# Pattern stage of a four-layer graph network: degrees as column sums on TensorE, five generators in flight in another order, mask buffers at other addresses

## The chip, the core and the metric

The kernel runs on one core of one Trainium2 chip. A core has TensorE (PE, with its weight loads listed apart as PEld), VectorE (DVE), ScalarE (ACT), GpSimd (POOL) and SyncE (SP), which here issues most transfers. The metric is the device time of one execution in microseconds, as the median of several runs.

## The reference, cut to what matters

The input is 16 graphs of 1024 nodes with 128 features each, and a sparse, symmetric adjacency matrix per graph. Four layers follow, each with a residual and a layer norm: graph attention, three SAGE convolutions on a thinned ("dilated") adjacency, and two plain graph products. The part that concerns us is the thinning, which goes row by row, since each row's removals change the later rows:

```python
def step(carry, n):
    row = jnp.take(carry, n, axis=0)
    nbi = row.astype(jnp.int32)
    num = jnp.sum(nbi)
    sf = jnp.where(num > T_DIL, (num + K_DIL - 1) // K_DIL, 1)
    rank = jnp.cumsum(nbi)
    rm = row & (rank % sf == 0)
    valid = (mask_b[n] != 0) & (num > 1)
    rm = jnp.where(valid, rm, False)
    keep = ~rm
    carry = carry.at[n].set(row & keep)
    carry = carry.at[:, n].set(carry[:, n] & keep)
    return (carry, None)
out, _ = jax.lax.scan(step, adj_bool, jnp.arange(N))
```

Here T_DIL is 10 and K_DIL is 2. The convolution then uses `adj * keep`, its row sums as degrees, three times with weights of its own and a batch norm over all nodes:

```python
deg = jnp.clip(jnp.sum(adj, axis=-1, keepdims=True), 1.0, None)
agg = jnp.einsum('bij,bjd->bid', adj, x) / deg
out = agg @ Wr + x @ Wx + b
```

## The kernel before

The program has four stages in one TileContext: `phase_att` (attention, layer 0), `phase_pattern` (the thinning), `phase_conv` (the three convolutions) and `phase_end` (layers 2 and 3). Memory is taken in pools. A pool opened after another one was closed gets the bytes of the closed one, and its tiles wait for the closed one's users. The code gives the order of instructions, but a planner that looks at the whole program with estimated times may let an instruction go ahead of older ones on its engine, within what the rings of buffers allow.

**Attention** writes for each graph a 0/1 mask of the adjacency in f16 (`MT` in SBUF, then `mask_d` in device memory, L261 to 272) and the layer's output `x1_d`, also transposed as `x1T_d`. `finish` of the last graph (L477) is the stage's tail. Its last steps are the reduction of `seen_z` into a flag (L589) and the stores of `x1_d` and `x1T_d` (L530 to L540).

**The pattern stage** uses that almost all nodes have few neighbours: of a sparse graph only nodes with 10 or more neighbours (candidates, at most 128 per graph) can lose edges. There are three kinds of generators.

- `find(b)`, one for each of 16 graphs, 11 yields. It loads the mask `m` (2 MB, a ring of three buffers, L726) and sums its rows on ACT with eight Relu instructions that accumulate (L730); that gives the degrees. POOL multiplies the eight diagonal blocks by a triangle (`md`, L734). Three times `earlier` follows (36 one-column matmuls, L744 and L748), with a comparison on DVE between, which finds the nodes that are small with respect to earlier ones. `slots` gives each candidate a slot and builds a one-hot `oh` (L700). `nodes` finds the node of each slot (8 matmuls, L710) and its indices (five operations on DVE, L713 to L717), and starts a gather of the nodes' features on POOL (L718). A second gather fetches the nodes' rows of the adjacency (`rows`, L776). Then come `pg` (64 matmuls, L785, the last readers of `m`) and `stay`, `le`, `l2` and `base` on DVE (L793 to L798), `pr` (L802) with RB, `early` and `num0` (L803 to L808), the transposes of the gathered rows (`pt`, L815) and their product with the one-hot (`pv`, L821, copied to `V`).
- `settle(g)`, one for eight graphs, 8 yields: five rounds that iterate the removals of eight graphs at once. Each is about ten tiny operations and three wide ones on DVE (L844 to L859), then eight one-column matmuls (L862). After them come the products `py` and `pk`, the edge weights `d`, and a store to `slots_d` (L912).
- `alone(b)`, one for each graph, 4 yields: ranks all nodes against the candidates (`prank`, 12 matmuls, L923), marks hits with two comparisons on DVE (`hit1` L928, `hit` L930), and finds small nodes whose edges are all gone, with `slots`, `nodes` and one more gather (L947).

The function `rolling(tasks, depth, lag)` (L624) writes these generators out in turns: one step of each that is active, in the order of their start. A further one starts when fewer than `depth` are active, the youngest has done `lag` steps, and those named as its conditions have ended. Before the change the call is `rolling(tasks, 3, 4)`. The list is: finds 0 to 7, settle 0, finds 8 to 15, settle 1, alones 0 to 7, alones 8 to 15 (which wait for settle 1).

PSUM is used through two rings of the stage: `ps` (four small tiles: all short sums, `pc`, `pr`, `pv`, `pn`) and `pb` (two wide tiles: `pg`, `pt`, `prank`, and the wide ones of `settle`).

**The convolution** starts on PE when its own pools are free and its first loads have landed; its first use of POOL is the power in `norm` (L1148).

Of the kernel before, what the change touches and what calls it, by code (L numbers as in the profile page):

```python
# [10 lines left out]
F32 = mybir.dt.float32  # L11
# [6 lines left out]
ALU = mybir.AluOpType  # L18
# [125 lines left out]
def phase_att(ctx, tc, t, c, x1_d, x1T_d, mask_d, flags):  # L144
# [13 lines left out]

    k_rank = load("k_rank", [P, E])
# [4 lines left out]
    k_id = load("k_id", [P, W])  # L164
    k_id_col = load("k_id_col", [P, 1])
    off_diag = cp.tile([P, W], F16, name="off_diag")
# [8 lines left out]
    w_all = cp.tile([P, 4 * F], F32, name="w_all")  # L175
    bias3 = cp.tile([P, 4 * F], BF16, name="bias3")
# [48 lines left out]

    MT = [cp.tile([P, NG, (NG - 1) * W + P], F16, name=f"mask{i}") for i in range(2)]
    for m in MT:
        nc.gpsimd.memset(m, 0.0)
    QS = [cp.tile([P, UNITS, C], F16, name=f"qs{i}") for i in range(2)]
    for q in QS:  # L230
        nc.gpsimd.memset(q, 0.0)
# [413 lines left out]
def phase_pattern(ctx, tc, t, c, mask_d, slots_d, x1_d, keep, flags):  # L645
# [5 lines left out]
    nc = tc.nc  # L651
    cp = ctx.enter_context(tc.tile_pool(name="q_c", bufs=1))
    mp = ctx.enter_context(tc.tile_pool(name="q_m", bufs=3))
# [6 lines left out]
    def load(name, shape, dtype=F16):  # L660
        w = cp.tile(shape, dtype, name=name)
        nc.sync.dma_start(w, t[name])
        return w
# [9 lines left out]
    node_col = node[:, :, 0]  # L673

# [7 lines left out]
    v2 = cp.tile([P, B], F32, name="v2")  # L682
    small = cp.tile([P, B, T], F16, name="small")
    seen_slots = cp.tile([P, 2 * B], F32, name="seen_slots")
# [7 lines left out]
    def slots(k, chosen, upto):  # L692
# [4 lines left out]
        slot = sm.tile([P, T], F16, name="slot")  # L697
# [6 lines left out]
        nc.vector.tensor_reduce(seen_slots[:, k : k + 1], slot, AX.X, ALU.max)  # L704
        return oh

    def nodes(k, oh, pc):
# [4 lines left out]
        at = sm.tile([P, 3], F32, name="at")  # L712
        nc.vector.tensor_scalar(at[:, 0:1], pc, -1.0, 0.0, op0=ALU.add, op1=ALU.max)  # L713
        nc.vector.tensor_scalar(at[:, 2:3], pc, 0.0, float(N), op0=ALU.is_equal, op1=ALU.mult)
        nc.vector.tensor_scalar(keep.index[:, k : k + 1], at[:, 0:1], float(k % B * N), None, op0=ALU.add)
        nc.vector.tensor_copy(keep.inner[:, k : k + 1], at[:, 0:1])
        nc.vector.tensor_tensor(keep.row[:, k : k + 1], at[:, 0:1], at[:, 2:3], ALU.add)  # L717
# [5 lines left out]
    def find(b):  # L723
# [3 lines left out]
        deg = sm.tile([P, T], F32, name="deg")  # L727
        for ti in range(T):
# [225 lines left out]
    for g in range(2):  # L954
        tasks += [(f"f{b}", find(b), []) for b in range(g * HALF, (g + 1) * HALF)]
        tasks.append((f"s{g}", settle(g), [f"f{b}" for b in range(g * HALF, (g + 1) * HALF)]))
        if g:
            tasks += [(f"a{b}", alone(b), []) for b in range(HALF)]
# [1206 lines left out]
```

## Time and profile before

| | us |
|---|---|
| median of 3 runs | 3310.53 (3309.57 to 3317.0) |
| profiled execution | 3305.06 |
| its span | 3303.3 |
| attention's last sums copied (L473) | 1711.4 |
| attention's last transposes done on PE | 1727.5 |
| first load of the pattern stage | 1734.9 |
| first `earlier` matmul (L748) | 1757.2 |
| settle 0, first operation and end | 1885.3, 1931.1 |
| settle 1, about, and end | 2045.5, 2091.7 |
| last `nodes` (L710) | 2182.4 |
| first product of the convolution (L1115) | 2191.4 |
| mean TensorE clock granted over the span | 0.917 |

Times on the profile's axis count from the start of the span. An idle time is put down to the event that came last before the engine went on; where the engine or tensor named had nothing to do with it, it was another. Busy times of PE include the pipelining of matmuls, so a share near 80% of PE means some 20% of real gaps, and a share of one engine over a stretch says nothing of which stage within it waits.

### The profile page before, as it was taken

To read this page: it belongs to the slowest core of one execution; us is meant where nothing else is said; L and a number is where in the kernel's file an instruction comes from. 1 tells how busy PE (TensorE), PEld (TensorE's weight loads), DVE (VectorE), ACT (ScalarE), POOL (GpSimd) and SP (SyncE) were. 2 spreads that over 40 slices of the span, in tenths; PEclk is the share of its full clock that TensorE was granted. 3 is DMA by queue.
4 is the path that set the end of the run, shared out by engine and by line. 5 is a ranking of instruction groups with operands and counts; after the bars stand their busy time and mean duration, and the time that the engine had idled before them with its cause. 6 is when DMAs were issued, how large, how long until landed. Compare 5 with 4: busy or idle time off the path is not lost. (4 is left out here: it accounts for less than half of the span.)

```text
span 3303.3 us, 68844 instructions
## 1 busy us (share of the span) xinstructions
PE 2837.5 (86%) x24700; PEld 2493.6 (75%) x24700; DVE 2312.2 (70%) x8374; ACT 1857.5 (56%) x5704; POOL 1351.8 (41%) x1302
## 2 busy tenths in 40 slices
PE   3999999999999999999975667567877799999997
PEld 1878887788877888778865666346766799999997
DVE  3788888888888888888763666755655466666665
ACT  1777777777777777777756733025645333333332
POOL 7655455554545545544023322133423333332221
PEclk7999999999999999999986867679989899999999
DMA  4422332223322233221015532034442444444341
GB/s 124 126 79 77 96 95 70 77 76 96 95 64 83 76 96 96 71 77 43 21 33 185 164 106 88 13 105 145 156 174 107 162 168 168 150 168 162 131 158 40
DMA packets 162014, 348.47 MB, mean 105 GB/s; under 512 B 14708, under 2 KB 68230, under 8 KB 161536
## 3 DMA queue, kind: packets, MB, share of 16 engines
q1 hardware_dynamic: 150912, 315.57, 29.9%
q0 software_dynamic: 10752, 28.42, 3.1%
q8 instruction: 197, 3.23, 0.4%
q14 instruction: 153, 1.25, 0.1%
HBM read 257.87 MB, written 87.03 MB: 104 GB/s over the span
## 5 line engine op out<-in xcount | busy, mean ns | idle before, releaser
L268 POOL TENSOR_SCALAR mask<-ld 104x1024 f16<-104x1024 f32 (+1 forms) x160 | 463.6, 2898 | 331.7 <-PE pg L428 170.9
L423 PE MATMUL pg<-parts,oh 104*128 104x384 f32 x1760 | 558.6, 392 | 0.3 <-ACT hg L442 0.2
L455 PE MATMUL pa<-hg,we 128*104 128x129 f32 (+1 forms) x3520 | 550.2, 274 | 3.5 <-ACT hg L442 2.3
L436 DVE SCALAR_TENSOR_TENSOR junk<-pg,w_a 128x128 f32<-128x128 f32 x1600 | 403.5, 284 | 204.0 <-PE pg L428 201.0
L442 ACT ACTIVATE hg<-pg,hg 128x128 f32<-128x128 f32 x1600 | 510.3, 369 | 16.5
L455 PEld LDWEIGHTS pa<-hg,we 128*104 128x104 f32 x3520 | 493.3, 173 | 22.2 <-ACT hg L442 10.4
L428 PE MATMUL pg<-parts,oh 104*128 104x384 f32 x1760 | 496.2, 353 | 0.0
L428 PEld LDWEIGHTS pg<-parts,oh 104*128 104x128 f32 x1760 | 320.4, 191 | 1.2
L423 PEld LDWEIGHTS pg<-parts,oh 104*128 104x128 f32 x1760 | 285.9, 192 | 28.4 <-issue 4.4
L440 ACT ACTIVATE hg<-sc 128x2 f32<-128x2 f32 (+1 forms) x880 | 186.7, 212 | 173.9 <-DVE junk L436 170.8
L410 DVE TENSOR_TENSOR we<-k_id,ids 128x832 f32<-128x832 f16 (+1 forms) x240 | 249.1, 1038 | 5.7 <-PE pa L455 3.6
L380 ACT CAST oh<-oh_b 104x1024 fp32r<-104x1024 bf16 (+1 forms) x240 | 223.2, 969 | 16.7 <-DVE oh_b L376 16.2
L1294 POOL TENSOR_TENSOR rstd<-ve,mhalf 128x4 f32<-128x4 f32 x96 | 97.0, 1011 | 326.2 <-DVE ve L1293 326.2
L287 PE MATMUL pw<-w_all,xT 128*104 128x512 f32 x320 | 178.8, 643 | 11.4 <-DMA xT<-in_xTp 8.9
L490 POOL TENSOR_TENSOR own<-parts 104x128 f32<-104x128 f32 x160 | 90.6, 600 | 220.4 <-DVE x_rows L510 208.7
L327 DVE TENSOR_TENSOR g<-k_slot,off 105x1408 f16<-105x1408 f16 x80 | 133.0, 1662 | 57.0 <-ACT off L323 57.0
L1298 DVE TENSOR_SCALAR x<-x,mv,rstd 128x128 f32<-128x128 f32 x256 | 106.9, 459 | 88.7 <-POOL rstd L1294 88.7
L376 DVE TENSOR_TENSOR oh_b<-pw,k_slot_edge 104x512 bf16<-104x512 f32 (+1 forms) x240 | 147.0, 636 | 9.5 <-PE pw L375 8.6
L348 ACT CAST qs<-pw 104x416 f16<-104x416 f32 (+1 forms) x240 | 114.6, 478 | 63.5 <-PE pw L345 62.2
L730 ACT ACTIVATE junk<-m 128x1024 bf16<-128x1024 f16 x128 | 133.6, 1048 | 29.2 <-POOL md L734 18.9
L355 DVE SCALAR_TENSOR_TENSOR one_way<-qs,mask 104x1040 bf16<-104x1040 f16 (+9 forms) x160 | 147.5, 922 | 1.1 <-POOL mask L270 0.7
L1403 ACT ACTIVATE y<-x,shift,rstd 128x128 f32<-128x128 f32 x128 | 52.7, 482 | 162.9 <-POOL shift L1396 162.9
(348 smaller groups left out, 6889.8 us busy)
## 6 DMA issues: line engine op xcount, KB each, us to landing
ld<-in_adjT SPq DMA_DIRECT2D x144, 416.0 KB
m<-mask_d SPq DMA_DIRECT2D x16, 2048.0 KB
keep_adj<-in_adjT SPq DMA_DIRECT2D x8, 4096.0 KB
adj<-in_adjT SPq DMA_DIRECT2D x8, 4096.0 KB
mask_d<-mask SPq DMA_DIRECT2D x144, 208.0 KB
hT_d<-uT SPq DMA_DIRECT2D x48, 512.0 KB
h<-hT_d SPq DMA_DIRECT2D x48, 512.0 KB
hT<-hT_d SPq DMA_DIRECT2D x32, 512.0 KB
```

Source lines behind the costliest of these rows:

```text
L268: nc.gpsimd.tensor_scalar(mt[:n, s, :N], ld[:n], 0.0, None, op0=ALU.is_gt)
L287: nc.tensor.matmul(pw[:W], xT[:, s * W : (s + 1) * W], w_all, start=True, stop=False)
L355: nc.vector.scalar_tensor_tensor(junk[:W, :nb, :], q[:W, at : at + nb, :W], EDGE, mt[:W, i, i * W : NP].rearrange("p (n w) -> p n w", w=W) ...
L376: nc.vector.tensor_tensor(o[:W, n0 : n0 + m, 1, :], pw[:W, :m, :], k_slot_edge[:W].unsqueeze(1).to_broadcast([W, m, C]), ALU.is_equal,)
L380: nc.scalar.copy(wide.ends[:W, n0 : n0 + m], o[:W, n0 : n0 + m])
L410: nc.vector.tensor_tensor(we[:, :n, :], k_id.unsqueeze(1).to_broadcast([P, n, W]), wide.ids[:, 2 * lo : 2 * hi].unsqueeze(2).to_broadcast( ...
L423: nc.tensor.matmul(flat[:, : 3 * F], own, d.parts[i][:W, p, :], start=p == 0, stop=False, skip_group_check=True,)
L428: nc.tensor.matmul(pg[:, 1:, :], other, reversed_parts(d.parts[j][:W, p, :]), start=False, stop=p == 1, skip_group_check=True,)
L436: nc.vector.scalar_tensor_tensor(junk, pg[:, 1 + e, :], 0.0, w_a2, op0=ALU.max, op1=ALU.mult, accum_out=d.sc[:, at + e : at + e + 1],)
L440: nc.scalar.activation(hg[:, u - lo, :ways, F], d.sc[:, at : at + ways], AF.Exp)
L442: nc.scalar.activation(hg[:, u - lo, e, :F], pg[:, 3 - 3 * e, :], AF.Copy, scale=hg[:, u - lo, e, F : F + 1])
L455: nc.tensor.matmul(PA[bank][:W, at : at + part.stop - part.start], we[:, 2 * (u - lo) + e, :], hg[:, u - lo, e, part], start=False, stop=T ...
```

## The change

Seven edits, all but the first and the last in `phase_pattern`:

- In attention, the tiles `MT` and `QS` come first in the constants' pool, then the constants that only the early part of a graph's work reads; `k_id` and those read to the end come after.
- The constants of the pattern stage go to a pool `q_k` of their own, and this and the masks' pool `q_m` (still three buffers) are opened first, so that they get the lowest addresses.
- `find` yields after the load. Then it forms the degrees as column sums of the mask on PE: for each of eight column blocks eight matmuls with a column of ones (64 in all), since the matrix is symmetric. One copy on ACT brings them to SBUF.
- `le` becomes eight Sign activations on ACT (values −1 and 1 in place of 0 and 1); `l2` carries twice the edge constant, and RB and `early` add `num0` and halve.
- In `alone`, `hit1` becomes a Sign on ACT. The slots of all calls are kept in one tile and checked at the end instead of one reduction per call.
- `nodes` keeps one operation on DVE in place of five. The others are done for eight graphs at once (`inner`), in `settle` and after the last `alone`; the gathers of features move to `alone` and to the end of the stage.
- The tasks' order is: finds 0 to 9, settle 0, then finds 10 to 15 alternating with alones 0 to 5, settle 1, alones 6 and 7, alones 8 to 15. The call is `rolling(tasks, 5, 2)`. The pools `late`, `xs` and `ahead` move to the other side of memory.

```diff
+    MT = [cp.tile([P, NG, (NG - 1) * W + P], F16, name=f"mask{i}") for i in range(2)]
+    for m in MT:
+        nc.gpsimd.memset(m, 0.0)
+    QS = [cp.tile([P, UNITS, C], F16, name=f"qs{i}") for i in range(2)]
...
     k_slot_edge = load("k_slot_edge", [P, C], F32)
-    k_id = load("k_id", [P, W])
     k_id_col = load("k_id_col", [P, 1])
+    w_all = cp.tile([P, 4 * F], F32, name="w_all")
+    bias3 = cp.tile([P, 4 * F], BF16, name="bias3")
...
+    k_id = load("k_id", [P, W])
...
+    kp = ctx.enter_context(tc.tile_pool(name="q_k", bufs=1))
+    mp = ctx.enter_context(tc.tile_pool(name="q_m", bufs=3))
     cp = ctx.enter_context(tc.tile_pool(name="q_c", bufs=1))
-    mp = ctx.enter_context(tc.tile_pool(name="q_m", bufs=3))
...
+    half_up = cp.tile([P, T], F32, name="half_up")
+    nc.vector.tensor_scalar(half_up, node_col, -1.0, 0.5, op0=ALU.mult, op1=ALU.add)
...
-        nc.vector.tensor_reduce(seen_slots[:, k : k + 1], slot, AX.X, ALU.max)
...
-        at = sm.tile([P, 3], F32, name="at")
-        nc.vector.tensor_scalar(at[:, 0:1], pc, -1.0, 0.0, op0=ALU.add, op1=ALU.max)
-        nc.vector.tensor_scalar(at[:, 2:3], pc, 0.0, float(N), op0=ALU.is_equal, op1=ALU.mult)
-        nc.vector.tensor_scalar(keep.index[:, k : k + 1], at[:, 0:1], float(k % B * N), None, op0=ALU.add)
-        nc.vector.tensor_copy(keep.inner[:, k : k + 1], at[:, 0:1])
-        nc.vector.tensor_tensor(keep.row[:, k : k + 1], at[:, 0:1], at[:, 2:3], ALU.add)
+        first = float(k % B * N)
+        nc.vector.tensor_scalar(
+            keep.index[:, k : k + 1], keep.node[:, k : k + 1], first - 1.0, first, op0=ALU.add, op1=ALU.max
+        )
+
+    def inner(k0, k1):
+
+        k = slice(k0, k1)
+        at = sm.tile([P, HALF], F32, name="at")
+        none = sm.tile([P, HALF], F32, name="none")
+        nc.vector.tensor_scalar(at, keep.node[:, k], -1.0, 0.0, op0=ALU.add, op1=ALU.max)
+        nc.vector.tensor_scalar(none, keep.node[:, k], 0.0, float(N), op0=ALU.is_equal, op1=ALU.mult)
+        nc.vector.tensor_copy(keep.inner[:, k], at)
+        nc.vector.tensor_tensor(keep.row[:, k], at, none, ALU.add)
+
+    def rows_of_x1(k):
         nc.gpsimd.indirect_dma_start(
             keep.xs[:, k, :], None, x1_d[k % B],
...
         nc.sync.dma_start(m, mask_d[b].rearrange("(t p) n -> p t n", p=P))
-        deg = sm.tile([P, T], F32, name="deg")
-        for ti in range(T):
-            junk = wp.tile([P, N], BF16, name="junk")
-            nc.scalar.activation(junk, m[:, ti, :], AF.Relu, accum_out=deg[:, ti : ti + 1])
-        yield
+        yield
+
+        pu = ps_s.tile([P, T], F32, name="pu", tag="ps")
+        for ni in range(T):
+            for ci in range(T):
+                nc.tensor.matmul(
+                    pu[:, ni : ni + 1], m[:, ci, ni * P : (ni + 1) * P], one, start=ci == 0, stop=ci == T - 1
+                )
+        deg = sm.tile([P, T], F32, name="deg", bufs=6)
+        nc.scalar.copy(deg, pu)
...
+        le = wp.tile([P, T, P], F16, name="le", bufs=3)
+        for ti in range(T):
+            nc.scalar.activation(le[:, ti, :], row, AF.Sign, bias=half_up[:, ti : ti + 1])
         yield
...
-        le = wp.tile([P, T, P], F16, name="le")
-        nc.vector.tensor_tensor(le, node_col.unsqueeze(2).to_broadcast([P, T, P]), row_b, ALU.is_le)
+        nc.vector.tensor_tensor(base[:, b], pg, stay, ALU.mult)
         l2 = L2[b % 2]
-        nc.vector.scalar_tensor_tensor(l2[:, :, :P], oh, EDGE, le, op0=ALU.mult, op1=ALU.add)
-        nc.vector.tensor_tensor(base[:, b], pg, stay, ALU.mult)
+        nc.vector.scalar_tensor_tensor(l2[:, :, :P], oh, 2 * EDGE, le, op0=ALU.mult, op1=ALU.add)
         yield
...
-        nc.vector.tensor_tensor(RB[:, b, :], pr[:, :P], less, ALU.mult)
+
+        nc.vector.tensor_copy(num0[:, b : b + 1], pr[:, P:])
+        nc.vector.scalar_tensor_tensor(
+            RB[:, b, :], pr[:, :P], num0[:, b : b + 1], half_less, op0=ALU.add, op1=ALU.mult
+        )
...
+        nc.vector.tensor_scalar(below[:, bs], v2[:, bs], -0.5, None, op0=ALU.add)
+        inner(g * HALF, (g + 1) * HALF)
...
         e1 = wp.tile([P, N], F16, name="hit1")
-        nc.vector.tensor_scalar(e1, pb, v1[:, b : b + 1], None, op0=ALU.is_equal)
+        nc.scalar.activation(e1, pb, AF.Sign, bias=below[:, b : b + 1], scale=-1.0)
         hit = wp.tile([P, N], F16, name="hit")
-        nc.vector.scalar_tensor_tensor(hit, pb, v2[:, b : b + 1], e1, op0=ALU.is_ge, op1=ALU.max)
+        nc.vector.scalar_tensor_tensor(hit, pb, v1[:, b : b + 1], e1, op0=ALU.is_equal, op1=ALU.is_ge)
         yield
...
         nodes(B + b, oh, pc)
+        rows_of_x1(b)
...
-    tasks = []
-    for g in range(2):
-        tasks += [(f"f{b}", find(b), []) for b in range(g * HALF, (g + 1) * HALF)]
-        tasks.append((f"s{g}", settle(g), [f"f{b}" for b in range(g * HALF, (g + 1) * HALF)]))
-        if g:
-            tasks += [(f"a{b}", alone(b), []) for b in range(HALF)]
+    tasks = [(f"f{b}", find(b), []) for b in range(HALF + 2)]
+    tasks.append(("s0", settle(0), [f"f{b}" for b in range(HALF)]))
+    for b in range(HALF - 2):
+        tasks += [(f"f{HALF + 2 + b}", find(HALF + 2 + b), []), (f"a{b}", alone(b), ["s0"])]
+    tasks.append(("s1", settle(1), [f"f{b}" for b in range(HALF, B)]))
+    tasks += [(f"a{b}", alone(b), ["s0"]) for b in (HALF - 2, HALF - 1)]
     tasks += [(f"a{b}", alone(b), ["s1"]) for b in range(HALF, B)]
-    rolling(tasks, 3, 4)
+    rolling(tasks, 5, 2)
+    inner(B, B + HALF)
+    inner(B + HALF, 2 * B)
+    for k in range(B, 2 * B):
+        rows_of_x1(k)
...
-    with tc.tile_pool(name="late", bufs=1) as lp:
+    with tc.tile_pool(name="late", bufs=1, side="right") as lp:
```

## The prediction

> **What bounds the kernel now.** The page comes first: the span, the engines' shares, and PE by slices.
>
> ```profile
> span 3303.3 us, 68844 instructions
> PE 2837.5 (86%) x24700; PEld 2493.6 (75%) x24700; DVE 2312.2 (70%) x8374; ACT 1857.5 (56%) x5704; POOL 1351.8 (41%) x1302
> ...
> PE   3999999999999999999975667567877799999997
> ...
> PEclk7999999999999999999986867679989899999999
> ```
>
> PE is at nine tenths everywhere except in slices 21 to 28. The first half of that dip is the pattern stage, the only one that the change rewrites. The chain of waits does not reach back so far (its longest pieces begin at 2478), so I read the stage by stretches. I cut them at the events that end each part: last work of attention, first `earlier` sum, start and end of settle 0 and of settle 1, last `nodes`.
>
> ```profile
> 1709.80:1734.90 25.10, 3.20 (x15) 2.19 (x14) 13.09 (x41) 2.82 (x8) 8.46 (x10) 0.61 0.15 42
> 1734.90:1757.20 22.30, 0.03 (x2) 0.13 (x2) 0.24 (x2) 8.70 (x17) 6.38 (x18) 0.50 0.90 310
> 1757.20:1885.30 128.10, 100.02 (x1762) 97.43 (x1762) 68.25 (x190) 90.99 (x176) 48.30 (x80) 0.79 0.51 162
> 1885.30:1931.10 45.80, 15.44 (x268) 14.53 (x268) 40.04 (x107) 14.68 (x29) 5.59 (x10) 0.57 0.07 26
> 1931.10:2045.50 114.40, 91.61 (x1591) 89.79 (x1590) 58.33 (x161) 60.08 (x117) 34.32 (x55) 0.80 0.43 139
> 2045.50:2091.70 46.20, 13.62 (x133) 10.73 (x132) 38.45 (x109) 1.96 (x4) 1.89 (x2) 0.57 0.01 2
> 2091.70:2182.50 90.80, 59.67 (x456) 31.07 (x454) 67.10 (x206) 2.29 (x16) 26.78 (x28) 0.67 0.06 16
> ```
>
> Columns: stretch, us, busy PE, PEld, DVE, ACT, POOL, then clock, DMA share, GB/s. Rows 3 and 5 are finds: PE 78 to 80% busy, 191.6 us for 16, 12.0 each. Rows 4 and 6 are settles: DVE 83 to 87%, PE nearly idle. Row 7 is 15 of the 16 alones: no engine over 74%, so a chain. Row 2 is a pure wait. What ended PE's waits:
>
> ```profile
> PE pn L862 <- DVE rm L859: 45.7, 10, 6.0
> PE pt L815 <- DMA rows<-in_adj,keep_index: 35.9, 13, 8.3
> PE pu L748 <- DMA diag<-in_diag_all: 29.6, 1, 29.6
> ```
>
> The third is the handover (PE's last work before it was at 1727.5; the name is that of the last event, not the cause). The timeline shows its steps, and SyncE's waits what held the first load:
>
> ```profile
> 1734.91 0.35 SPq L662 DMA_DIRECT2D q_less<-in_q_less  x1
> 1748.08 3.10 POOL L734 TENSOR_TENSOR md<-m,q_less 128x128 f16<-128x128 f16 x8 [13.01 <-DMA m<-mask_d]
> 1756.95 0.17 DVE L736 TENSOR_SCALAR s<-deg 128x8 f16<-128x8 f32 x1 [21.76 <-ACT junk L730]
> 1757.17 0.17 PE L748 MATMUL pu<-s,md 128*128 128x1 f16 x1 [29.65 <-DMA diag<-in_diag_all]
> ```
>
> ```profile
> SPq L726 <- PE pg L785: 187.9, 13, 21.9
> SPq L662 <- DMA x1T_d<-x1T: 58.3, 1, 58.3
> ```
>
> The constants waited for attention's very last store, the mask took until 1748.1, and eight Relu sums on ACT until 1756.95.
>
> **The change, part by part.**
>
> *Handover.* By the tile sizes in the code, the old constants lay on the first mask buffer, long idle by 1700, and still waited for that store: the wait is for whole released pools. The new `q_k` and `q_m` hold 54,272 bytes, which lie inside attention's constants pool; its last reader is the `seen_z` reduction (L589, ending 1721.8). So loading starts about 1722, not 1734.9. The work pools still wait for the store. Six constants at 0.47 us and 10.2 us (issue 1737.9 to `md` 1748.1) put mask 0 at 1735. Degrees become 64 one-column matmuls; `earlier` does 36 in about 1.0 us, so 1.8 us, and with the copy (0.16) and `s` (0.17) 2.5 us instead of 8.9, beside `md` (3.1). First sum at 1738.3 if the store lands as now. It now shares the DMA engines with 6 MB of masks, which I charge with 3 us: 1741, a gain of **16**. Bounds: 19 (no delay) and 6 (mask unchanged at 1748.1, first sum at 1751).
>
> *Sixteen finds.* Now: V copies at 1814.86, 1829.55 and 1844.66 give 14.9 us per find, of which PE works 12.0 and waits mainly for the gathered rows (35.9/13 = 2.8). Removed: eight Relu (1.04 each) on ACT, `le` (1.22), the slot reduction (0.15) and four index operations (0.15 each) on DVE. None bounds; 0. Added on ACT: eight Signs with a bias operand, bounded by 0.26 (`row`, no operand) and 0.48 us (L1403, two operands), 2.1 to 3.8 us against 8.4 removed; hidden beside `pg`. Added on PE: 1.8 us, not hidden. PE then needs 13.8 of every 14.9 us. Five finds in flight put more PE work between `pc` and `pt` (issue and landing of the rows take about 6 us), which should hide most of that wait; I keep the period at 14.8. Bounds: 13.8 (PE alone) and 16.7 (waits stay 2.9).
>
> *Settle 0.* It starts after ten finds instead of eight, with only the end of two finds and the front of a third (about 18 us of PE) beside it. At the same place now, `earlier` of find 8 ran at 1912.3 although its `s` and `md` were done by 1883.4: PE takes the short sums in the code's order, behind the five rounds. So I expect the same hole, about 46 us, plus some DVE work of its companions.
>
> *Six alones among the finds.* 59.67/15 = 4.0 us of PE each, 24 us, added to a PE that is nearly full. The count for sixteen finds, settle 0 and six alones: when settle 0 begins, eight finds are through and some 6 us of PE work of the next two is done, 8×13.8+6 = 116 us, divided by 0.93 (13.8/14.8) 125, with 6 to fill the pipe 131; from 1741 that is 1872. Settle 0 with 10 us of its companions' DVE, 56: 1928, with ten finds done and the eleventh up to its `pg`. Then 8 us of that, 5×13.8+24 = 93 more, over 0.93, 109; drain 7: 2044. That is 303 us instead of 288.3, a loss of **15**. Bounds from the period's (16 times −1.0 and +1.9): a gain of 1, a loss of 45. On SyncE's queue the slots store stands between the loads of masks; if find 11's mask waits behind it, 9.6 us once, inside these bounds. On POOL an `md` that waits for its mask holds back the next find's gather of rows, as it does now.
>
> *Settle 1* has two alones beside it (now one): 46 + 2, a loss of **2** (0 to 7, two alones' DVE).
>
> *Alones after settle 1.* Eight instead of 15. Now 90.8/15 = 6.05 each: with a lag of 4 in a generator of 5 steps they hardly overlap. With a lag of 2, `hit1` (1.28 on DVE) becomes a Sign of 1024 columns on ACT, 1.05 (L730, no operand) to 1.24 (L1086, two). The last `nodes` in the trace, whose ranks were done, follow each other every 3.43 us; I take 4.5, between that and 6.05 and nearer to the chain, plus 7 us for the last one's own chain: 43 instead of 90.8, a gain of **48**. Bounds: 8×3.43+7 = 34 and 8×6.05+7 = 55.
>
> *Gathers moved to the end.* 16 of 0.99 us on POOL, eight of them possible before the last alone; the others take 8×1.3 = 10 us. POOL's first task in the next stage comes 17 us after the last `nodes` (L1148 at 2199.72), so 0; 10 if that cover is gone. The batched index operations (eight of 0.15) are 1 us on DVE, off the path. The rest (other sides of memory, order of loads at the start, where SP issues 0.43 us pieces) 0: attention's first matmul waits for weights that come later than `k_id`.
>
> The Trainium skill ("ScalarE: Activation LUTs", Rules for kernel authors) sends plain arithmetic to VectorE, "up to about 3× faster" per element in bf16, which speaks against the Signs. Here the PSUM compare took 1.28 us on DVE and the nearest ACT rows 1.05 to 1.24; by the rule `hit1` would be an estimated 3.8 us on ACT and the tail up to 8×2.5 = 20 us longer. The rows decide.
>
> PE's clock falls where it idles; one `pg` block took 3.73 us in the flow and 5.39 after settle 0:
>
> ```profile
> 1875.29 3.73 PE L785 MATMUL pg<-oh,m 128*128 128x128 f16 x64
> 1930.14 5.39 PE L785 MATMUL pg<-oh,m 128*128 128x128 f16 x64
> ```
>
> Both settles stay, so I take no gain from a warmer clock; the clock of rows 3 and 5 (0.79, 0.80) is in the 12.0.
>
> **Sum.** −16 + 15 + 2 − 48 = −47 us. The profiled execution took 3305.06 (span 3303.3 and 1.8 around it), so 3258; the three timed runs have a median of 3310.53, 5.5 above it, so **3263.5**. The bounds of the finds (−16 to +30 around their term) dominate; with 8 us for all others, added in squares, the likeliest case spans 3245 to 3295.
>
> **Rivals.**
>
> *R1, slower: PE waits for masks.* Now ACT and POOL wait for a mask (POOL's `md` 33.7 us in four times between 1790 and 1885) and PE never does. The degree matmuls sit in PE's stream, and PE takes the short sums in the code's order. Three mask buffers serve five finds: find b+3 loads when `pg` of find b ends, and find to find that load took 9.6 us (`pg` end 1818.9, `md` 1828.6). In the code only 1.4 us of sums stand between. If nothing else fills, 8.2 us × 13 reloads = 107 us: 3370. It decides from 47/13 = 3.6 us per find. Queued behind the waiting sums are the older find's `pr` and the next one's `pc`, and with them DVE's `RB` and POOL's gather. Against it: `pg` and `pt` are let ahead (11 matmuls of a `pg` ran at 1826.33 before an older `pv`), 5.2 us of filling; and from find 11 on finds start four steps apart with an alone between, so masks are early.
>
> *R2, PE the bound at a worse rate:* waits stay 2.9 on top of 13.8, 1.9×16 = 30 lost: 3293. For: everything added lands on PE. Against: the rows' wait is what five in flight cover.
>
> *R3, better:* the finds run at PE's 13.8, −16, and the tail at its bound of 34, −9: 3238. For: 4.0 us of PE and 67.10/15 − 1.28 = 3.2 of DVE per alone allow it. Against: the settles' hole leaves PE cold each time.
>
> *R4, masks not early:* if the wait is still the store, the handover gains 6: 3273. For: the first load waited exactly for it. Against: that wait was seen with other neighbours in memory.
>
> **How the numbers follow.** Likeliest 0.49, R4 0.12, R2 0.13, R3 0.10, R1 0.13, sums that cancel to within 0.2% (6.6 us, about what the timed runs can tell) 0.03. Faster 0.84, same 0.03, slower 0.13. The range reaches from R3's far side, 3230, to beyond R2, 3298; outside lie R1, no change and a few hundredths of tails.
>
> **What would show it.** First `q_less` near 1722 and first `earlier` near 1741 (R4: 1735 and 1751). No Relu sums on ACT; PE about 1.8 us more per find. V copies 14 to 15 us apart; PE waiting for `m<-mask_d` by less than 1 us per find (R1: over 4). Settle 0 about 50 us, the last `nodes` 43 us after the second slots store, next stage's first matmul near 2144. I am wrong if the finds' period leaves 13.8 to 16.7, or the tail keeps 6 us per alone.

## The result, and the profile after

The changed kernel takes 3261.22 us (median of 4 runs, 3255.18 to 3274.36) against 3310.05 us for the kernel before on the same chip. The ratio is 0.9865, with a 95% interval of 0.9817 to 0.9914: faster by 1.3%. Forecast were 3263.5 us and faster. The total was right, but two of the reasons behind it were wrong; the experiments show which. The kernels further down were timed in sets, each set with the kernel before beside it (medians 3303.40 to 3311.40), so across sets their ratios to before are compared, not their microseconds.

The page of the kernel after, span, busy times and the two rows of slices:

```profile
span 3262.6 us, 70599 instructions
PE 2852.2 (87%) x25724; PEld 2516.6 (77%) x25724; DVE 2277.8 (70%) x8203; ACT 1785.6 (55%) x5608; POOL 1357.1 (42%) x1302
...
PE   3999999999999999999995859567877799999997
...
PEclk7999999999999999999996778788988899999999
```

The dip is still in slices 21 to 28, but three slices of its first half are now fuller: the 21st, 23rd and 25th stand at 9, 8 and 9, where they stood at 7, 6 and 7. The stretches of the stage, cut at the same events as before (attention's last sums, first load, first `earlier`, about the end of find 7, slots store of settle 0, last V copy, slots store of settle 1, last `nodes`; columns as in the prediction):

```profile
1717.60:1728.40 10.80, 0.00 (x0) 0.00 (x0) 10.44 (x31) 0.17 (x2) 2.81 (x2) 0.56 0.00 0
1728.40:1748.70 20.30, 4.62 (x76) 3.74 (x77) 3.84 (x15) 1.51 (x4) 7.13 (x13) 0.50 0.85 300
1748.70:1893.00 144.30, 122.58 (x2569) 119.61 (x2569) 61.86 (x163) 42.70 (x120) 55.13 (x94) 0.75 0.50 166
1893.00:1957.50 64.50, 35.72 (x511) 33.82 (x510) 50.05 (x116) 12.67 (x33) 14.68 (x27) 0.69 0.25 84
1957.50:2061.70 104.20, 93.18 (x1716) 83.06 (x1714) 63.53 (x157) 34.68 (x85) 32.22 (x43) 0.87 0.32 102
2061.70:2106.50 44.80, 10.79 (x125) 8.27 (x125) 35.48 (x99) 3.60 (x6) 8.75 (x9) 0.56 0.04 9
2106.50:2144.50 38.00, 24.48 (x246) 14.32 (x244) 25.91 (x65) 9.94 (x17) 7.77 (x9) 0.81 0.06 19
```

PE works 85% of the third stretch (122.58 of 144.30) and 89% of the fifth. Settle 0 (fourth) is longer than before, 64.5 us, and PE is idle for 28.8 of them. The last row holds eight alones.

Attention ends at 1717.6, where it ended at 1711.2 in the profile of before. Its code is the same in all the kernels below but for the places of some tiles, and its last sums came between 1710.2 and 1725.9 in them. So I read the stage from that event on. One table holds every profile; the times are us, all from the instructions named above ("end" is the load of the slots for the next stage, right after the last `nodes`):

| kernel | handover: last sums to first `earlier` | finds and settle 0: to the last V copy | settle 1: to its store | tail: to the end | stage |
|---|---|---|---|---|---|
| before | 46.0 | 291.1 | 43.4 | 90.8 | 471.3 |
| after | 31.1 | 313.0 | 44.8 | 38.4 | 427.4 |
| degrees_twice | 31.5 | 342.8 | 44.9 | 38.7 | 457.8 |
| degrees_on_act | 39.7 | 324.6 | 44.9 | 38.6 | 447.8 |
| settle_ring | 31.5 | 312.8 | 45.9 | 37.2 | 427.4 |
| hit1_on_dve | 31.5 | 319.7 | 46.6 | 48.5 | 446.3 |
| old_order | 30.9 | 276.5 | 42.5 | 70.7 | 420.6 |
| waits_by_tile | 25.2 | 299.2 | 46.6 | 38.1 | 409.2 |
| settle_later | 31.2 | 286.3 | 46.4 | 43.2 | 407.2 |
| two_masks | 31.1 | 384.3 | 46.5 | 37.0 | 498.9 |
| hit1_alone | 46.0 | 295.8 | 42.5 | 64.6 | 448.9 |
| degrees_alone | 39.4 | 269.8 | 43.2 | 87.7 | 440.0 |
| later_and_by_tile | 25.2 | 291.9 | 47.9 | 42.5 | 407.4 |
| three_finds_later | 25.2 | 268.3 | 45.2 | 67.1 | 405.8 |

The alones stand in different columns: after has six among the finds, two beside settle 1 and eight in the tail; before, old_order, hit1_alone and degrees_alone have fifteen in the tail; by their matmuls, settle_later and later_and_by_tile have some nine there and three_finds_later some fourteen. Where the code of a stretch is the same, two profiles differ by some us (the finds of before and hit1_alone, 291.1 and 295.8; the tails of before and degrees_alone, 90.8 and 87.7), so smaller differences say nothing.

From before to after the stage lost 43.9 us: -14.9, +21.9, +1.4 and -52.4. Attention gave 6.4 back, and the rest of the program after the stage took 1117.6 instead of 1120.8: 40.7 us in the span.

The handover, in the timeline of after (only the lines that carry it):

```profile
1727.94 0.28 DVE L589 TENSOR_REDUCE flags<-seen_z 128x1 f32<-128x160 f32 x1
1728.42 0.35 SPq L663 DMA_DIRECT2D q_less<-in_q_less  x1
1731.18 10.45 SPq L743 DMA_DIRECT2D m<-mask_d  x3
...
1740.64 0.33 ACT L538 COPY x1T<-pw 128x208 f32<-128x208 f32 x1 [6.69 <-DMA x1T_d<-x1T]
...
1747.43 0.39 DVE L676 TENSOR_SCALAR half_up<-q_node 128x8 f32<-128x8 f16 x1 [14.00 <-DMA x1T_d<-x1T]
```

The first load goes out 0.5 us after the `seen_z` reduction, 10.8 us after attention's last sums instead of 23.7. But then the masks fill the DMA engines (0.85 busy, 300 GB/s in the second stretch), so attention's last piece of `x1T` waits 6.69 us for a buffer, and the store that the work pools wait for lands about 29.4 us after the last sums, not 23.7. What ended PE's waits in the finds and settle 0 of after:

```profile
PE pn L890 <- DVE rm L887: 15.2, 4, 4.9
PE pt L843 <- DMA rows<-in_adj,keep_index: 14.6, 8, 4.9
PE pu L749 <- DMA m<-mask_d: 4.8, 2, 4.2
```

PE waits for masks by 4.8 us in all, 0.3 per find.

### The profile page after: what moved, and what is told of

It reads as the page before. It is cut to its first block, busy times and chain, and to the rows that moved or that the text cites. A ratio compares the mean times of both kernels' runs of the same rounds, so it can differ in the third digit from the quotient of the medians.

```text
span 3262.6 us, 70599 instructions
## 1 busy us (share of the span) xinstructions
PE 2852.2 (87%) x25724; PEld 2516.6 (77%) x25724; DVE 2277.8 (70%) x8203; ACT 1785.6 (55%) x5608; POOL 1357.1 (42%) x1302
## 3 DMA queue, kind: packets, MB, share of 16 engines
q1 hardware_dynamic: 150912, 315.57, 30.4%
q14 instruction: 151, 1.24, 0.1%
## 5 line engine op out<-in xcount | busy, mean ns | idle before, releaser
L380 ACT CAST oh<-oh_b 104x1024 fp32r<-104x1024 bf16 (+1 forms) x240 | 223.2, 969 | 15.7 <-DVE oh_b L376 15.3
L376 DVE TENSOR_TENSOR oh_b<-pw,k_slot_edge 104x512 bf16<-104x512 f32 (+1 forms) x240 | 147.1, 635 | 10.1 <-PE pw L375 9.3
L369 ACT CAST oh_b<-pw 104x512 bf16<-104x512 f32 (+1 forms) x240 | 133.0, 555 | 18.3 <-PE pw L368 18.2
```

What stands on the lines that cost most here:

```text
L380: nc.scalar.copy(wide.ends[:W, n0 : n0 + m], o[:W, n0 : n0 + m])
```

## The experiments

The first question was whether TensorE bounds the finds, and what each part of the change is worth in the changed kernel.

**degrees_twice.** Every degree sum done twice.

```diff
-        for ni in range(T):
+        for _ in range(2):
+            for ni in range(T):
...
```

> The changed kernel with every degree sum done twice on TensorE (same output): 64 more one-column matmuls per find, 28.7 us of PE in all by the 28.7 us that the 1024 existing ones take. Theory (PE is what the finds wait for, so added PE work shows nearly whole): the stretch from the first `earlier` sum to the last V copy grows from 313 us by 22 to 29, the whole from 3261 to about 3286. Rival (the stretch is set by waits for gathered rows, masks and settle 0, and PE work is absorbed in the 61 us that PE stands idle there): growth under 10 us, about 3266.

Measured: 3298.79 us, ratio to before 0.9965 (0.9948 to 0.9982). The finds' stretch took 342.8 us, 29.8 more, for 28.7 us of added sums. In the order of the changed kernel added PE work shows whole. The first theory stands. (The whole grew by 37.6 us, more than the 25 expected; the stage gives 30.4 of them.)

**degrees_on_act.** Degrees back on ScalarE, in the changed kernel.

```diff
-                nc.tensor.matmul(
-                    pu[:, ni : ni + 1], m[:, ci, ni * P : (ni + 1) * P], one, start=ci == 0, stop=ci == T - 1
-                )
...
-        nc.scalar.copy(deg, pu)
...
+            nc.scalar.activation(junk, m[:, ti, :], AF.Relu, accum_out=deg[:, ti : ti + 1])
```

> The changed kernel with the degrees back on ScalarE (eight Relu sums of 1.04 us per find, as before the change; one junk buffer in place of two), all else as changed. Theory (PE bounds the finds; ACT is busy 43 of 144 us there and takes 8.4 us more per find): PE loses 28.7 us, the finds' stretch falls from 313 us to 288-298; the handover gives back 6 us, since the first `s` waits for eight Relus; the whole 3261 - 10 to 20, so 3241 to 3251. Rival (with five finds in flight ACT becomes the bound, 8.4 + 4.3 us of every 14.7 and the Signs and copies queue behind the Relus): the stretch is 313 or longer, the whole 3261 to 3290.

Measured: 3284.69 us, 0.9917 (0.9891 to 0.9944), some 23 us slower than after. The finds took 324.6 us although PE had 22 us less to do (229.1 busy instead of 251.5), and the handover grew to 39.7. PE's first wait of this run, up to find 7:

```profile
PE pu L765 <- DVE s L753: 48.0, 6, 23.3
```

`s` is made from the degrees; the finds now start two steps apart, and their Relus queue up on ACT, which was busy for 216.9 us of the stretch instead of 90.0. The rival stands: with five finds in flight and the Relus back, the finds wait for ScalarE. The row of the handover also splits that term: the earlier loading 46.0 to 39.7, the degrees on TensorE 39.7 to 31.1.

**hit1_on_dve.** The compare of the alones back on VectorE.

```diff
-        nc.scalar.activation(e1, pb, AF.Sign, bias=below[:, b : b + 1], scale=-1.0)
+        nc.vector.tensor_scalar(e1, pb, v2[:, b : b + 1], None, op0=ALU.is_ge)
...
```

> The changed kernel with `hit1` of the alones back on VectorE, a compare of 1024 PSUM columns of about 1.28 us, in place of the Sign of 1.11 us on ScalarE. Theory (VectorE is busy 25.9 of the 38 us of the last eight alones, so the step belongs on ScalarE, but the chain is shortened by the lag of 2 far more than by this): the last eight alones take 40 to 44 us instead of 38, the finds' stretch grows by 0 to 6, the whole 3261 + 2 to 10. Rival (the Sign is what shortened the tail from 6.05 us per alone): the tail goes back to 48 us or more. Rival (plain compares belong on VectorE): the tail falls under 37.

Measured: 3269.41 us, 0.9883 (0.9857 to 0.9909). Its tail (that of after is the last row of the stretches above):

```profile
2123.70:2172.20 48.50, 29.19 (x246) 16.46 (x244) 35.46 (x76) 1.44 (x9) 7.69 (x9) 0.68 0.05 15
```

The tail took 10.1 us more, eight times 1.26, as if nothing of the compare's 1.28 us were hidden. But 4.7 of the 10.1 are PE's: the same 246 matmuls took 29.19 us at a clock of 0.68, and 24.48 at 0.81 in after. I had expected 40 to 44 for the tail. The lag of 2 was in place, and an alone cost 6.06 us again, as in the kernel before. The rival stands, against the prediction. (The finds were 6.7 us longer in this profile; the medians differ by 8 us in all, so I give that part no cause.)

**settle_ring.** The counts of the settles' rounds in a PSUM buffer of their own.

```diff
-    ps_s = ctx.enter_context(tc.tile_pool(name="q_ps", bufs=4, space=PSUM))
+    ps_s = ctx.enter_context(tc.tile_pool(name="q_ps", bufs=3, space=PSUM))
...
-            pn = ps_s.tile([P, HALF], F32, name="pn", tag="ps")
+            pn = ps_s.tile([P, HALF], F32, name="pn", tag="st", bufs=1)
```

> The changed kernel with the counts of the settles' rounds (pn of 8 columns) in a PSUM buffer of their own, and three instead of four buffers left for the finds' short sums. Theory (settle 0 empties PE because short sums are taken in the code's order, so find 10's degrees stand behind four rounds): during the rounds PE does the next finds' sums, the 18 us of PE waiting for `rm` in settle 0 fall under 8, and the stretch of 313 us shrinks by 8 to 18, the whole to about 3248. Rival (the hole comes from DVE, which the rounds fill, or from the start order of the finds): no change in that wait, and the whole at 3261, up to 3275 for want of the fourth buffer.

Measured: 3259.77 us, 0.9851 (0.9825 to 0.9878), no change. The theory was half right. PE in settle 0, first after, then settle_ring: the degrees of find 10 (`pu<-q_run,m`), its `pc`, the settle's transpose (`pt<-ident,d`), and find 10's `pg`:

```profile
1932.14 1.84 PE L749 MATMUL pu<-q_run,m 128*128 128x1 f16 x64
...
1952.83 1.03 PE L793 MATMUL pc<-oh,q_node 128*128 128x128 f16 x8 [3.67 <-DVE oh L708]
1954.49 1.94 PE L940 MATMUL pt<-ident,d 128*128 128x128 f32 x8 [0.44 <-DVE keep_index L720]
1956.22 4.51 PE L812 MATMUL pg<-oh,m 128*128 128x128 f16 x64
```

```profile
1913.98 1.74 PE L749 MATMUL pu<-q_run,m 128*128 128x1 f16 x64
1923.52 0.71 PE L793 MATMUL pc<-oh,q_node 128*128 128x128 f16 x5 [3.33 <-DVE oh L708]
...
1946.23 1.94 PE L940 MATMUL pt<-ident,d 128*128 128x128 f32 x8 [4.36 <-DVE d L937]
1947.97 5.77 PE L812 MATMUL pg<-oh,m 128*128 128x128 f16 x64
```

The degrees moved from 31.6 to 18.7 us after find 7's V copy, as they should. But `pg` started right after the settle's `pt`, as before. By the code, the settle's `py`, `pk` and `pt` share the two large PSUM buffers with `pg`, so the wait seems to have moved to the next shared buffer; no run gave `pg` a buffer of its own.

**settle_later.** So I changed the order instead: settle 0 stands after twelve finds, while four are in flight.

```diff
-    tasks = [(f"f{b}", find(b), []) for b in range(HALF + 2)]
+    tasks = [(f"f{b}", find(b), []) for b in range(HALF + 4)]
...
-    for b in range(HALF - 2):
+    for b in range(HALF - 4):
...
```

> The changed kernel with settle 0 after twelve finds in the order instead of ten (so that four finds, not two, are in flight when it starts), four alones among the finds and twelve after settle 1. Theory (settle 0 empties PE because the order has drained the finds by then): 10 to 20 us of PE's idle time in settle 0 go, the stretch from the first `earlier` to the last V copy falls from 313 to 285-297 (8 us of it the two alones that left), the tail grows by four alones of about 4.7, of which two left the finds and two the time beside settle 1: 48 to 58 us instead of 38; the whole 3261 - 0 to 12. Rival (find 10's `pg` waits for the settle's own large PSUM tiles, as the run with a ring for the counts showed, whatever the order): the stretch falls only by the 8 us, and the whole gets slower by 2 to 10.

Measured: 3239.25 us, 0.9810 (0.9783 to 0.9837). The finds' stretch fell by 26.7 us, of which the two alones that left it are an estimated 8 (twice PE's 4.0); PE's idle time in it fell from 61.5 to 44.9 us. The tail grew by only 4.8, to 43.2, where I had expected 48 to 58. The theory stands: with the settle after ten finds, the order itself had drained the pipe.

**old_order.** Everything of the change but the order: eight finds, settle 0, eight finds, settle 1, alones; three in flight, four steps apart.

```diff
-    tasks = [(f"f{b}", find(b), []) for b in range(HALF + 2)]
...
-    rolling(tasks, 5, 2)
+    rolling(tasks, 3, 4)
```

> The changed kernel with the old order of the stage: finds 0-7, settle 0, finds 8-15, settle 1, sixteen alones, three generators in flight, each started four steps after the one before. Degrees, `hit1` and the early masks stay as changed. Theory (the order is worth the tail: alones at a lag of 4 hardly overlap): handover 31 us from attention's last sums; finds and settle 0 without alones 291 to 310 us (29 us of degree sums on PE, of which the 81 us that PE stood idle before hide a part); after the second slots store 15 alones of 4.8 to 5.5 us, 72 to 83 us; the whole 3285 to 3300. Rival (the alones became short because `hit1` moved to ScalarE, not by the lag): 15 alones at 4.0, 60 us, and the whole under 3280.

Measured: 3252.43 us, 0.9844 (0.9815 to 0.9873). The finds were faster than either expectation (276.5 us against 291 to 310), the tail lay between theory and rival, and the whole is on the rival's side. Its windows, finds 1 to 7 and the tail:

```profile
1774.90:1871.70 96.80, 87.19 (x1764) 85.20 (x1762) 58.85 (x126) 34.80 (x96) 42.62 (x68) 0.89 0.59 193
2068.90:2139.60 70.70, 47.43 (x456) 26.91 (x453) 48.44 (x128) 18.29 (x31) 22.35 (x22) 0.81 0.06 16
```

Fifteen alones at the old lag took 70.7 us, 4.7 each, as in the changed kernel (38.4 for eight, 4.8). And three finds in flight keep PE 90% busy at 13.8 us per find. Both orders leave PE the same wait for the gathered rows in finds and settle 0 (14.4 us in old_order, 14.6 in after, 35.9 in the kernel before), so five in flight hide no more of it than three. The order of the change as a whole, with five in flight, the lag of 2, the alones among the finds and settle 0 after ten finds, brought nothing that can be measured: the stage is 6.8 us shorter without it. The place of settle 0 is part of that. settle_later, timed in the same set, keeps five in flight, the lag of 2 and four alones among the finds; its stage is 13.4 us shorter than old_order's, and each of its four times (3232.99 to 3242.19) lies below each of old_order's (3245.10 to 3259.85).

**hit1_alone and degrees_alone.** The two parts that were left, each put into the kernel before by itself.

```diff
-        nc.vector.tensor_scalar(e1, pb, v1[:, b : b + 1], None, op0=ALU.is_equal)
+        nc.scalar.activation(e1, pb, AF.Sign, bias=below[:, b : b + 1], scale=-1.0)
...
```

> The kernel before with one edit: `hit1` of the alones as a Sign on ScalarE instead of a compare on VectorE (and the small `below` it needs). Theory (the alones are a chain through VectorE, and 1.28 us fewer on it is 1.28 us fewer per alone, whatever the lag): the 15 alones after the second slots store take 69 to 74 us instead of 90.8, the whole 20 us less, a ratio of 0.993 to 0.995. Rival (my prediction's: with a lag of 4 in a generator of 5 steps the alones hardly overlap, so the lag must fall first): 85 to 91 us, since the Sign of 1.11 us takes the compare's place in the chain.

Measured: 3283.27 us, 0.9917 (0.9895 to 0.9940). Its tail:

```profile
2098.70:2163.20 64.50, 44.21 (x456) 26.89 (x453) 49.62 (x191) 19.05 (x30) 26.85 (x28) 0.90 0.09 23
```

The tail fell from 90.8 to 64.6 us with the lag untouched, more than the 19 that 1.28 us for each of 15 give. The row shows more than a shorter chain: the same 456 matmuls kept PE busy for 44.2 us at a clock of 0.90, where they took 59.67 at 0.67 before (busy time times clock is 40 in both), and PE's idle time fell from 31.1 to 20.3, its wait for `lone` on VectorE alone from 9.2 to 1.4. In every profile here the tail's clock is 0.67 to 0.71 with the compare on VectorE (before, degrees_alone, hit1_on_dve) and 0.77 to 0.90 with the Sign.

```diff
-            nc.scalar.activation(junk, m[:, ti, :], AF.Relu, accum_out=deg[:, ti : ti + 1])
...
+                nc.tensor.matmul(
+                    pu[:, ni : ni + 1], m[:, ci, ni * P : (ni + 1) * P], one, start=ci == 0, stop=ci == T - 1
+                )
...
```

> The kernel before with one edit: the degrees as column sums on TensorE instead of eight Relu sums on ScalarE. Theory (with three finds in flight PE's added 1.8 us per find are covered by its waits, and ScalarE's queue no longer holds `oh32`, `turned` and the V copies behind Relus that wait for a mask): the first `earlier` sum comes 37 to 40 us after attention's last sums instead of 46, finds and settle 0 take 277 to 285 us instead of 291, V copies 13.8 to 14.3 us apart instead of 14.8; the whole 12 to 22 us less. Rival (my prediction's: Relus cost nothing, PE's 1.8 us per find land on the path where the wait for the rows stays): 291 to 320 us, the whole 5 us less to 20 us more.

Measured: 3279.70 us, 0.9918 (0.9890 to 0.9946). The finds and settle 0 took 269.8 us, better than the theory's 277 to 285. Finds 1 to 7 of the kernel before, then of this one (V copy to V copy):

```profile
1784.00:1887.40 103.40, 81.50 (x1417) 79.29 (x1414) 58.39 (x159) 71.96 (x139) 38.90 (x62) 0.83 0.56 181
```

```profile
1773.70:1867.00 93.30, 83.09 (x1763) 81.40 (x1760) 60.23 (x163) 18.27 (x39) 42.39 (x70) 0.94 0.64 209
```

PE did some 12.6 us more work (seven times 1.8) in 1.6 us more busy time, at a clock of 0.94 instead of 0.83, and its idle time fell from 21.9 to 10.2. Up to find 7 its wait for the gathered rows fell from 16.4 to 8.8 us, as if the degree sums filled it. `turned`, which before started 1.1 to 2.4 us after its transposes in three of seven finds, behind Relus, now starts 0.1 us after them every time. How much the added sums, the removed Relus and the clock each give was not separated, nor whether the clock would be as high in every run.

**two_masks.** The price of rival R1, with a mask buffer taken away.

```diff
-    mp = ctx.enter_context(tc.tile_pool(name="q_m", bufs=3))
+    mp = ctx.enter_context(tc.tile_pool(name="q_m", bufs=2))
```

> The changed kernel with two mask buffers instead of three. Theory (PE did not wait for masks because a third buffer lets each load run a find ahead): with two, find b+2 can load only after `pg` of find b, the load of 9.6 us and the degree sums then stand in PE's stream, PE waits for `m` by 3 to 9 us per find instead of 0.3, and the stretch of 313 us grows by 40 to 130. Rival (the large sums let ahead fill such waits whatever the number of buffers): under 15 us.

Measured in a single run: 3336.25 us, finds 384.3 us, 71 more. PE's first wait in that stretch:

```profile
PE pu L749 <- DMA m<-mask_d: 57.3, 9, 9.1
```

The mechanism of R1 is real. The third buffer holds it off, not the large sums let ahead.

**waits_by_tile.** The two early pools wait for the users of their own bytes only.

```diff
-    kp = ctx.enter_context(tc.tile_pool(name="q_k", bufs=1))
-    mp = ctx.enter_context(tc.tile_pool(name="q_m", bufs=3))
+    kp = ctx.enter_context(tc.tile_pool(name="q_k", bufs=1, reuse_waits="tile"))
+    mp = ctx.enter_context(tc.tile_pool(name="q_m", bufs=3, reuse_waits="tile"))
```

> The changed kernel with the constants' and masks' pools waiting only for the users of their own bytes in attention's memory, not for the whole released pool. Theory (the first mask landed 13.8 us after its issue because it shared the DMA engines with attention's last stores, and delayed these): loading starts before attention's last sums (now 10.8 us after them), masks lie ready, the last store lands about 24 us after the last sums as it did before the change (29.4 now), and the first `earlier` sum comes at 24 to 27 us instead of 31.1: 4 to 7 us off the whole, about 3255. Rival (the wait is the same with either rule): first constant at 10.8 us, no change.

Measured: 3245.24 us, 0.9819 (0.9788 to 0.9849). Loads and `x1T` in its timeline (attention's last sums are at 1719.2):

```profile
1683.25 0.58 SPq L663 DMA_DIRECT2D q_less<-in_q_less  x1
1695.84 6.99 SPq L743 DMA_DIRECT2D m<-mask_d  x3
```

```profile
1737.26 0.33 ACT L538 COPY x1T<-pw 128x208 f32<-128x208 f32 x1 [1.67 <-DMA x1T_d<-x1T]
```

The masks are in place before attention ends, the last piece of `x1T` waits 1.67 us instead of 6.69, the last store lands some 23.5 us after the last sums instead of 29.4, and the first `earlier` comes 25.2 us after them. The theory stands, sharing included. The finds were also 13.8 us shorter in this profile; for that I have no cause, and the next run does not repeat it.

**later_and_by_tile and three_finds_later.** Two attempts to beat both kernels. The first joins the edits of settle_later and waits_by_tile; the second keeps the pools by tile and has another order:

```diff
+    tasks = [(f"f{b}", find(b), []) for b in range(HALF + 3)]
+    tasks.append(("s0", settle(0), [f"f{b}" for b in range(HALF)]))
+    tasks += [(f"f{b}", find(b), []) for b in range(HALF + 3, B)]
+    tasks.append(("s1", settle(1), [f"f{b}" for b in range(HALF, B)]))
...
+    rolling(tasks, 4, 3)
```

> The changed kernel with settle 0 after twelve finds and the two pools waiting by tile, both together. If the two gains are of different places (idle PE in settle 0; the handover), they add: first `earlier` at 25 us after attention's last sums, the stage from there to the last node 401 us instead of 427, the whole 3230 to 3240, a ratio to before of 0.975 to 0.979. If the finds that start earlier only wait longer later: 407 us, 0.981.

> The changed kernel with pools waiting by tile and another order: finds 0-10, settle 0, finds 11-15, settle 1, then all alones; four generators in flight, each started three steps after the one before. Theory (three finds already fill PE, the five in flight bring nothing, and alones after settle 1 cost 4.7 us each, little more than the 4.0 us of PE that they cost among the finds): finds 13.8 us apart, 16 finds and settle 0 in 255 to 270 us, settle 1 45, thirteen to sixteen alones 61 to 75; the stage 395 to 412 us, a ratio to before of 0.972 to 0.981. Rival (the alones among the finds were free): 415 to 430 us, 0.982 to 0.988.

Measured: 3236.17 us, 0.9778 (0.9746 to 0.9810), and 3238.14 us, 0.9783 (0.9754 to 0.9813). Both beat the changed kernel, and they can't be told apart. In the profiles the two gains of the first do not add (stage 407.4, settle_later 407.2); in the timed runs they may. The finds of the second are 15.2 us apart, not 13.8, though PE hardly waits. Two windows of it:

```profile
1781.00:1801.00 20.00, 20.00 (x338) 19.85 (x338) 10.75 (x22) 6.83 (x21) 9.74 (x18) 0.71 0.49 161
1841.00:1861.00 20.00, 20.00 (x330) 19.85 (x327) 9.49 (x27) 7.42 (x23) 8.34 (x12) 0.67 0.50 164
```

PE is busy for all of the 20 us, at a clock of 0.71 and 0.67. From the V copy of find 0 to that of find 7 it was busy for 106.1 of 106.8 us at 0.73, where old_order has 87.2 of 96.8 at 0.89: busy time times clock is 77 and 78, so the lower clock is enough for the longer period. That the first attempt, with alones among the finds, and the second, with all of them after settle 1, come out equal fits that the place of the alones brings little.

## Why the prediction was right, and where it was not

*Handover, -16: right (-14.9).* The load left with the `seen_z` reduction, as reasoned; R4 falls. The first `earlier` was forecast at 1741 on an axis where attention ends at 1711.2; taken from there it came at 1742.3. I charged 3 us for the shared DMA engines; the last store came 5.7 us later than before. waits_by_tile shows that the sharing was the price. (The 2.5 us for sums, copy and `s` were more than the three prices given, which add to 2.1; `md`, with its 3.1 beside them, set the step all the same.)

*Finds, settle 0 and six alones, +15: the size was short (+21.9), and its parts were wrong.* "Removed: eight Relu ... None bounds; 0" failed: in the old order, moving the degrees alone takes 21 us off this stretch, with less waiting for the rows and a higher PE clock, and in the new order putting the Relus back makes it 11.6 us longer although PE has 22 us less to do. "Five finds in flight ... should hide most of that wait" named the wrong cover: three did as well, with the same edits. The V copies of finds 0 to 7 are 14.8 us apart in the mean, as forecast, but not one by one: finds 1 to 4 come 9 to 13 apart, then there is a gap of 34. Of the three pieces in the count, the time to settle 0 was 131 us and took 144.3, settle 0 was 56 and took 64.5, and the rest was 116 and took 104.2. PE was not "nearly idle" in the settles of before either: rows 4 and 6 have it busy for 34 and 29%. I named the hole and its first cause; that find 10 starts late by the order, and that its `pg` shares buffers with the settle, I did not see. settle_later won back some 19 us of it.

*The rivals.* PE waits 0.3 us per find for masks, under the bound of 1 that I had set; two_masks shows that the third buffer keeps R1 away, where I had named the large sums let ahead. Of R2 something was true: in the order of the changed kernel added PE work does land on the path (degrees_twice), and the finds lost more than forecast. R3's tail of 34 us was not reached (38.4).

*Settle 1, +2: right (+1.4).*

*Alones, -48: the size was right (-52.4), the step wrong.* "With a lag of 4 in a generator of 5 steps they hardly overlap" failed: at that lag they take 4.3 to 4.7 us once `hit1` is off VectorE, and at a lag of 2 they take 6.06 with it on. I had priced the Sign only against the compare (1.05 to 1.24 against 1.28; it took 1.11) and not asked what VectorE's queue did meanwhile: for 15 alones it was busy 67.1 of 90.8 us, and the compare stood ahead of the other alones' operations. In one cycle of that trace it ran from 2137.75 to 2139.03 before an `oh` whose slots had been written by 2137.84. "I take no gain from a warmer clock" failed in the tail too: its clock went from 0.67 to 0.81. How much of the tail's gain is the shorter queue and how much the clock is not separated, since both came with the Sign in every run. That only eight alones were left in the tail gained little: together with settle 0's place, the six among the finds cost what they had saved, as old_order shows.

On the Trainium skill ("ScalarE: Activation LUTs", Rules for kernel authors): the rule for VectorE would have made the tail up to 20 us longer by the estimate; here the move to ScalarE made it 10.1 us shorter. The measurement decides for this place. The rule's factor is for bf16; this compare reads f32 from PSUM, and there the two engines took 1.28 and 1.11 us, so the estimated 3.8 was too high. And the rule compares one operation, while the gain lay in VectorE's queue and PE's clock.

*Gathers at the end, 0: right.* The next stage's first matmul came at 2153.31, 9.3 us after the last `nodes` sums began; 9.4 before. It waits for weights in both.

So the total hit because errors of both signs met, and that it came within 2.3 us of the median is luck: the four timed runs lie 19 us apart. By the runs, the stage gains 31 us from the degrees alone, 22 from `hit1` alone and 6 from the early memory. These do not add up (all three with the rest, in the old order, give 51), and the new order gives 0 to 7 back.

## What to carry to other kernels

When an in-order engine feeds a chain of short steps, price an operation moved off it by what queues behind it, not only by its duration against its twin's on the other engine. Before you credit an order of tasks with a gain, ask what the old order would do with the other edits, and look for shared buffers one after another: freeing the first may only move the wait to the next. And price what an edit takes away as well as what it adds: 28.7 us of further sums cost 29.8 in the changed kernel, so sums on PE were not free there, and yet putting the first such sums in place of the Relus shortened the stage by 20.4 us in that order (degrees_on_act against after) and by 31.3 in the old one.

## What the runs showed of the hardware

PE's granted clock mattered more than I had allowed for. The same 456 matmuls took 59.67 us of PE time at a clock of 0.67 and 44.21 at 0.90, after 1.28 us of VectorE work per alone was taken away. Nor does the same code always get the same clock: finds 1 to 7 of hit1_alone, in which nothing was changed, took 110.8 us at 0.78, where those of the kernel before took 103.4 at 0.83.

```profile
1786.30:1897.10 110.80, 83.83 (x1419) 81.38 (x1415) 61.04 (x163) 71.79 (x139) 41.85 (x62) 0.78 0.55 171
```

And a PE that is busy throughout does not always get the full clock: two stretches of 20 us in three_finds_later ran at 0.67 and 0.71. The finds hold many matmuls of one column; whether these are why was not tried. Attention, whose code differs between the kernels only in the places of some tiles, ended up to 15.7 us apart in the profiles (1710.2 to 1725.9), so a single span can't show a part of this change; the stage, cut at its own events, can.
